# Layer boundary of a two-layer interaction network: grouped statistics, first operand spread by 0/1 matmuls, three keep-alive matmuls

## The chip, the cores and the metric

One core of a Trainium2 chip. The metric is the device time of one execution in microseconds (us), smaller is better; medians of several executions. All runs told here are of the same (fast) state. "Granted clock" is the share of TensorE's full clock that its throttle lets through, as the profile records it. DVE is VectorE, ACT ScalarE, PE TensorE, PEld its weight loads, SPq the queue from which SyncE issues DMAs.

## The reference, cut to what matters

```python
def _batchnorm(h, gamma, beta):                       # over rows and embedding
    mean = jnp.mean(h, axis=(0, 2), keepdims=True)
    var = jnp.var(h, axis=(0, 2), keepdims=True)
    return (h - mean) * rsqrt(var + EPS) * gamma + beta

def _cin_layer(out, x, W, b, gamma, beta):            # x: 4096 rows, 32 fields, 16
    h = einsum('rne,rfe->rnfe', out, x).reshape(r, -1, e)   # all products of pairs
    h = einsum('rce,oc->roe', h, W) + b
    return _batchnorm(h, gamma, beta)

h1 = _cin_layer(x, x, W1, b1, g1, beta1)              # 128 channels
out, direct1 = h1[:, :64], h1[:, 64:]
direct2 = _cin_layer(out, x, W2, b2, g2, beta2)
return concatenate([direct1, direct2], axis=1).sum(axis=-1)
```

The normalization of layer 1 needs the statistics of all of layer 1, so nothing of layer 2 can be multiplied before the last tile of layer 1 is done. The change is about this boundary.

## The kernel before

128 tiles of 512 columns per layer. In each tile VectorE multiplies two operands into z, TensorE multiplies z by the weights (fp32, two passes per matmul: 4096 passes recorded for layer 2's 2048 matmuls), ScalarE evicts the result, VectorE takes statistics. Layer 1's h (64 channels kept) stays in on-chip memory. At the boundary, all 128 tiles' statistics are aggregated by one instruction, and layer 2 takes its first operand a from h by DMA, one row spread over eight partitions:

```python
mv = const.tile([P, 2], ...)
nc.vector.bn_aggr(mv, stats.rearrange("p a b -> p (a b)"))   # 128 tiles x 6 numbers
...                                    # scale and shift: eight small steps
normalize(0)                           # ScalarE, h of the first tile
...
for t in range(NT):                    # layer 2
    b = bpool.tile([P, 4 * T], ...)
    nc.sync.dma_start(b, ...)          # 1 MB from HBM
    for i in range(4):
        a = apool.tile([P, T], ...)
        nc.sync.dma_start(a, src.unsqueeze(1).to_broadcast([16, 8, T]))   # from h
        z = zpool.tile([P, 4, T], ...)
        nc.vector.tensor_tensor(z, a (broadcast), b, ALU.mult)
        for k in range(4):
            nc.tensor.matmul(ps, w2_sb[:, m, :], z[:, k, :], ...)
```

The pools of layer 1 are closed before those of layer 2 are opened, so layer 2's buffers lie on memory that layer 1 has used, and wait for its last use (4.5 us on layer 1's last matmul, by the waits list). The first pool opened is that of layer 1's weights, and the first one of layer 2 lies where it lay:

```python
wpool = ...  # layer 1's weights
lpool = ...  # layer 1's loads
rpool = ...
...          # layer 2, later:
bpool = ...  # lies on wpool and lpool
```

## Time and profile before

| | before |
|---|---|
| time, median of 6 | 2289.79 us (2288.67 to 2290.40) |
| last matmul of layer 1 to first of layer 2 | 16.2 us |
| from there to the eviction of layer 2's first tile | 17.0 us, where a steady tile takes 13.73 |
| first tile's eviction to last tile's eviction of layer 2 | 1744.1 us |
| last tile's eviction to the end | 16.1 us |

The lines are shown in the prediction; in a timeline, the columns are start, duration, engine, line, operation, count, and in square brackets how long the engine stood idle before and what ended that.

### The profile page before, as it was taken

How to read it: one execution, taken by the hardware profiler on the slowest of the kernel's cores; microseconds unless marked ns; L12 is line 12 of the kernel's file. 1: busy time of each engine (PE TensorE's matmuls, PEld its weight loads, DVE VectorE, ACT ScalarE, POOL GpSimd, SP SyncE). 2: the span in 40 equal slices, each digit the busy share in tenths (PEclk: the TensorE clock that was granted, in tenths of full speed). 3: DMA queues.
4: the chain of work that ended last, by engine and by line, in shares of the span. 5: the costliest groups of instructions: out<-in, count | busy, mean ns of one | idle time of the engine just before them, and what ended most of it. 6: DMA issues, size and time to landing. Idle time of an engine off the chain costs nothing.

```text
span 2288.8 us, 15238 instructions
## 1 busy us (share of the span) xinstructions
PE 2245.0 (98%) x5376; PEld 982.4 (43%) x5376; DVE 1750.0 (76%) x1129; ACT 398.7 (17%) x580; POOL 2.3 (0%) x5
## 2 busy tenths in 40 slices
PE   8999999979999999999999999999999999999997
PEld 3444444434444444444444444444444444444443
DVE  6888888877777777777777777777777777777776
ACT  3555555556000000000000000000000000000000
POOL 0000000000000000000000000000000000000000
PEclk9999999989999999999999999999999999999998
DMA  8888888868888888888888888888888888888883
GB/s 316 298 305 295 298 292 301 296 201 158 153 150 151 153 154 155 155 150 151 153 157 155 154 150 151 152 158 154 154 150 151 152 159 154 154 149 151 152 155 92
DMA packets 132428, 417.05 MB, mean 182 GB/s; under 512 B 14848, under 2 KB 14848, under 8 KB 115456
## 3 DMA queue, kind: packets, MB, share of 16 engines
q1 hardware_dynamic: 131616, 413.20, 81.7%
q10 hardware_dynamic: 736, 2.89, 0.4%
q8 instruction: 42, 0.69, 0.1%
q14 instruction: 34, 0.28, 0.0%
HBM read 278.66 MB, written 3.15 MB: 123 GB/s over the span
## 4 chain that ended last, share of the span: by engine, by line
PE 77%; issue 22%; DVE 0%; ACT 0%; POOLq 0%; ACTq 0%; DVEq 0%
PE ps L211 77%; ACT h L177 0%; DVE mv L60 0%; POOLq L276 0%; ACTq L182 0%; DVE d L224 0%; DVEq L276 0%; ACT e L213 0%; DVE stats L214 0%; DVE d L215 0%; DVE ss L72 0%; DVE c L69 0%; ACT sd L64 0%; DVE r L66 0%; DVE ss L75 0%
## 5 line engine op out<-in xcount | busy, mean ns | idle before, releaser
L211 PE MATMUL ps<-z,w_sb 128*128 128x512 f32 x4096 | 1761.1, 593 | 16.2 <-ACT h L177 16.2
L208 DVE TENSOR_TENSOR z<-a,b 128x2048 f32<-128x2048 f32 x512 | 1173.0, 2291 | 446.4 <-PE ps L211 439.5
L211 PEld LDWEIGHTS ps<-z,w_sb 128*128 128x128 f32 x4096 | 779.2, 190 | 998.1 <-issue 980.8
L163 PE MATMUL ps<-z,w_sb 128*128 128x512 f32 x1024 | 450.9, 598 | 3.2 <-DVE z L151 3.2
L213 ACT ACTIVATE e<-ps,bn_sb 128x512 f32<-128x512 f32 x128 | 87.9, 687 | 1635.0 <-PE ps L211 1624.0
L151 DVE TENSOR_TENSOR z<-a,b 128x2048 f32<-128x2048 f32 x128 | 293.4, 2292 | 68.9 <-PE ps L163 65.0
L163 PEld LDWEIGHTS ps<-z,w_sb 128*128 128x128 f32 x1024 | 193.0, 191 | 259.6 <-issue 251.0
L129 ACT ACTIVATE e<-ps,bn_sb 128x512 f32<-128x512 f32 x128 | 87.9, 687 | 219.5 <-PE ps L163 219.5
L214 DVE BATCH_NORM_STATS2 stats<-e 128x6 f32<-128x512 f32 x128 | 87.7, 685 | 5.3 <-ACT e L213 5.3
L132 DVE BATCH_NORM_STATS2 stats<-e 128x6 f32<-128x512 f32 x128 | 87.8, 686 | 3.4 <-ACT e L129 3.4
L130 ACT ACTIVATE ed<-ps,bn_sb 64x512 f32<-64x512 f32 x128 | 87.4, 683 | 3.2
L131 ACT ACTIVATE h<-ps,bn_sb 64x512 f32<-64x512 f32 x128 | 87.2, 681 | 2.4
L215 DVE TENSOR_REDUCE d<-e 128x32 f32<-128x512 f32 x128 | 85.5, 668 | 0.0
L177 ACT ACTIVATE h<-h,keep 128x512 f32<-128x512 f32 x64 | 45.7, 800 | 3.8 <-issue 1.9
L161 PE MATMUL ps<-zr,w_sb 32*128 32x512 f32 x256 | 37.4, 655 | 8.1 <-DVE w_sb L115 8.1
L135 DVE TENSOR_REDUCE d<-ed 128x32 f32<-128x512 f32 x64 | 42.8, 668 | 0.0
L161 PEld LDWEIGHTS ps<-zr,w_sb 32*128 32x128 f32 x256 | 10.2, 186 | 31.7 <-issue 23.5
L148 DVE TENSOR_TENSOR zr<-r 128x512 f32<-128x512 f32 x16 | 10.9, 682 | 6.7 <-DMA r<-in_xr 6.7
L60 DVE BATCH_NORM_AGGREGATE mv<-stats 128x2 f32<-128x768 f32 x2 | 7.2, 3612 | 0.0
L129 ACT ACT_TABLE_LOAD x1 | 1.3, 1283 | 8.5 <-DMA bn_sb<-in_bn 8.5
L224 DVE TENSOR_SCALAR d<-d,ss 128x2048 f32<-128x2048 f32 x2 | 2.6, 1343 | 0.0
L180 POOL TENSOR_SCALAR d<-d,direct 128x2048 f32<-128x2048 f32 x1 | 2.0, 2048 | 503.3 <-DVE direct L174 503.3
(17 smaller groups left out, 6.7 us busy)
## 6 DMA issues: line engine op xcount, KB each, us to landing
b<-in_xb SPq DMA_DIRECT2D x128, 1024.0 KB, 7.2
a<-h SPq DMA_DIRECT2D x512, 256.0 KB, 5.2
a<-in_xa SPq DMA_DIRECT2D x128, 512.0 KB, 4.9
b<-in_xb SPq DMA_DIRECT2D x128, 512.0 KB, 5.6
r<-in_xr SPq DMA_DIRECT2D x16, 512.0 KB, 6.1
out<-d SPq DMA_DIRECT2D x2, 1024.0 KB, 4.5
w_sb<-in_w ACTq DMA_DIRECT2D x1, 1024.0 KB, 10.0
out<-d ACTq DMA_DIRECT2D x2, 512.0 KB, 8.9
```

What stands on the lines that cost most here:

```text
L129: nc.scalar.activation(e, ps, AF.Identity, bias=b1)
L130: nc.scalar.activation(ed[to, :], ps[KEEP:, :], AF.Identity, bias=b1[KEEP:])
L131: nc.scalar.activation(hs[c][to, :], ps[:KEEP, :], AF.Identity, bias=b1[:KEEP])
L132: nc.vector.bn_stats(stats1[:, t, :], e)
L151: nc.vector.tensor_tensor(z, a.rearrange("p (a t) -> p a t", a=2).unsqueeze(2).to_broadcast([P, 2, 2, T]), b.rearrange("p (b t) -> p b t", ...
L161: nc.tensor.matmul(ps, w1_sb[rows, 4 + s // 4, :], zr[rows, :], start=True, stop=False)
L163: nc.tensor.matmul(pss[t], w1_sb[:, m, :], z[:, m // 2, m % 2, :], start=False, stop=(m == 3))
L208: nc.vector.tensor_tensor(z, a.unsqueeze(1).to_broadcast([P, 4, T]), b, ALU.mult)
L211: nc.tensor.matmul(ps, w2_sb[:, m, :], z[:, k, :], start=(m == 0), stop=(m == 15))
L213: nc.scalar.activation(e, ps, AF.Identity, bias=b2)
L214: nc.vector.bn_stats(stats2[:, t, :], e)
L215: nc.vector.tensor_reduce(d2[half][:, c * RT : (c + 1) * RT], e.rearrange("p (r e) -> p r e", e=EMB), AX.X, ALU.add,)
```

## The change

Its intent: shorten the path between the layers and at the end. Statistics are aggregated per 16 tiles, so that only a short aggregation is left at the end; the last tile's statistics come straight from PSUM; the small steps are fewer; the first tile's four a are made by TensorE itself, by matmuls with a 0/1 matrix of 64 rows into PSUM (called spreads below), in place of a DMA; three matmuls whose result is not used (keep-alive) are to keep the array's clock up; the direct sums are scaled later.

```diff
+        def add(self, t, h, bias=None):
+            ...
+            nc.vector.bn_stats(self.stats[:, t % SG, :], h)
+            ...
+            if t % SG == SG - 1:
+                nc.vector.bn_aggr(self.groups[:, t // SG, 1:3], self.stats...)
...
+    running = psum.tile([P, T], FP, tag="ps", name="running")
+    for k in range(3):
+        nc.tensor.matmul(running, w2_sb[:, k, :], w2_sb[:, 0:4, :]..., start=True, stop=True)
...
-    normalize(0)
-    nc.gpsimd.tensor_scalar(d1, d1, direct[:, 0:1], direct[:, 2:3], ALU.mult, ALU.add)
+    nc.vector.tensor_scalar(hs[0][low, :], hs[0][low, :], ss1[low, 0:1], ss1[low, 1:2], ...)
...
+    def spread(i):
+        a = psum.tile([P, T], FP, tag="ps", name="a_first")
+        return nc.tensor.matmul(a, select[:, i]..., hs[0][low, :], start=True, stop=True)
+    spread(0)
...
+            if t == 0:
+                a = spreads[i]
+                if i == 0:
+                    spread(1)
+            else:
+                nc.sync.dma_start(a, src.unsqueeze(1).to_broadcast([16, 8, T]))
+            for js in ([slice(0, 1), slice(1, 4)] if t == 0 and i == 0 else [slice(0, 4)]):
...
+                if t == 0 and m in (0, 3):
+                        spread(2 + m // 3)
```

`low` is partitions 0 to 63. A square root of a constant at the very start loads ScalarE's table early (1.28 us).

More of the change, by code (lines that the diff above doesn't have):

```diff
@@ L38 @@
 GROUP = 8
+SG = 16
 @with_exitstack
@@ L47, in tile_cin @@
     sums = ctx.enter_context(tc.tile_pool(name="sums", bufs=1))
+    spool = ctx.enter_context(tc.tile_pool(name="spool", bufs=2))
     epool = ctx.enter_context(tc.tile_pool(name="epool", bufs=2))
@@ L55, in load_bn @@
         return bn_sb
-    def batchnorm(stats, gamma, beta, n):
-        mv = const.tile([P, 2], FP, tag=f"mv{n}", name=f"mv{n}")
-        nc.vector.bn_aggr(mv, stats.rearrange("p a b -> p (a b)"))
-        ve = const.tile([P, 1], FP, tag=f"ve{n}", name=f"ve{n}")
-        nc.vector.tensor_scalar(ve, mv[:, 1:2], EPS, None, ALU.add)
-        sd = const.tile([P, 1], FP, tag=f"sd{n}", name=f"sd{n}")
-        nc.scalar.activation(sd, ve, AF.Sqrt)
-        r = const.tile([P, 1], FP, tag=f"r{n}", name=f"r{n}")
-        nc.vector.reciprocal(r, sd)
-        c = const.tile([P, 1], FP, tag=f"c{n}", name=f"c{n}")
-        nc.vector.tensor_scalar(c, r, r, ve, ALU.mult, ALU.mult)
-        nc.vector.tensor_scalar(c, c, -0.5, 1.5, ALU.mult, ALU.add)
-        ss = const.tile([P, 3], FP, tag=f"ss{n}", name=f"ss{n}")
-        nc.vector.tensor_scalar(ss[:, 0:1], r, c, gamma, ALU.mult, ALU.mult)
-        ms = const.tile([P, 1], FP, tag=f"ms{n}", name=f"ms{n}")
-        nc.vector.tensor_tensor(ms, mv[:, 0:1], ss[:, 0:1], ALU.mult)
-        nc.vector.tensor_tensor(ss[:, 1:2], beta, ms, ALU.subtract)
-        nc.vector.tensor_scalar(ss[:, 2:3], ss[:, 1:2], float(EMB), None, ALU.mult)
-        return ss
+    eps = const.tile([P, 1], FP, tag="eps", name="eps")
@@ new lines, in tile_cin, with __init__, scale_shift @@
+    nc.vector.memset(eps, EPS)
+    nc.scalar.activation(const.tile([P, 1], FP, tag="sd", name="table"), eps, AF.Sqrt)
+    class Stats:
+        def __init__(self, n):
+            self.n = n
+            self.groups = const.tile([P, NT // SG, 3], FP, tag=f"groups{n}", name=f"groups{n}")
+            nc.vector.memset(self.groups, 1.0)
+        def add(self, t, h, bias=None):
+            if t % SG == 0:
+                self.stats = spool.tile([P, SG, 6], FP, tag="stats", name=f"stats{self.n}")
+            nc.vector.bn_stats(self.stats[:, t % SG, :], h)
+            if bias is not None:
+                means = self.stats[:, t % SG, 1:5:3]
+                nc.vector.tensor_scalar(means, means, bias, None, ALU.add)
+            if t % SG == SG - 1:
+                nc.vector.bn_aggr(self.groups[:, t // SG, 1:3], self.stats.rearrange("p a b -> p (a b)"))
+        def scale_shift(self, gamma, beta):
+            mv = const.tile([P, 2], FP, tag="mv", name="mv")
+            nc.vector.bn_aggr(mv, self.groups.rearrange("p a b -> p (a b)"))
+            sd = const.tile([P, 1], FP, tag="sd", name="sd")
+            root = nc.scalar.activation(sd, mv[:, 1:2], AF.Sqrt, bias=eps)
+            half_ve = const.tile([P, 1], FP, tag="ve", name="half_ve")
+            nc.vector.tensor_scalar(half_ve, mv[:, 1:2], EPS, 0.5, ALU.add, ALU.mult)
+            r = const.tile([P, 1], FP, tag="r", name="r")
+            nc.vector.reciprocal(r, sd)
+            c = const.tile([P, 1], FP, tag="c", name="c")
+            nc.vector.tensor_scalar(c, r, r, half_ve, ALU.mult, ALU.mult)
+            nc.vector.scalar_tensor_tensor(c, c, 1.5, r, ALU.subtract, ALU.mult, reverse0=True)
+            ss = const.tile([P, 3], FP, tag=f"ss{self.n}", name=f"ss{self.n}")
+            nc.vector.tensor_tensor(ss[:, 0:1], c, gamma, ALU.mult)
+            nc.vector.scalar_tensor_tensor(
+                ss[:, 1:2], mv[:, 0:1], ss[:, 0:1], beta, ALU.mult, ALU.subtract, reverse1=True
+            )
+            return ss, root.ins
@@ L80, in tile_cin @@
+    select = const.tile([KEEP, 4, 16, 8], FP, tag="select", name="select")
+    nc.gpsimd.memset(select, 1.0)
+    nc.gpsimd.affine_select(
+        out=select,
+        in_=select,
+        pattern=[[-16, 4], [-1, 16], [0, 8]],
+        compare_op=ALU.is_equal,
+        fill=0.0,
+        base=0,
+        channel_multiplier=1,
+    )
     hs = [hpool.tile([P, T], FP, tag=f"h{c}", name=f"h{c}") for c in range(NC)]
     d1 = sums.tile([P, ROWS // 2], FP, tag="sum", name="d1")
-    stats1 = const.tile([P, NT, 6], FP, tag="stats", name="stats1")
+    stats1 = Stats(1)
@@ L127, in finish, with evict_direct, sum_direct @@
             ed = eds[c]
-            e = epool.tile([P, T], FP, tag="e", name="e")
-            nc.scalar.activation(e, ps, AF.Identity, bias=b1)
-            nc.scalar.activation(ed[to, :], ps[KEEP:, :], AF.Identity, bias=b1[KEEP:])
+            if t == NT - 1:
+                stats1.add(t, ps, b1)
+            else:
+                e = epool.tile([P, T], FP, tag="e", name="e")
+                nc.scalar.activation(e, ps, AF.Identity, bias=b1)
+                stats1.add(t, e)
             nc.scalar.activation(hs[c][to, :], ps[:KEEP, :], AF.Identity, bias=b1[:KEEP])
-            nc.vector.bn_stats(stats1[:, t, :], e)
+            if t == NT - 1:
+                return ps
+            evict_direct(ed[to, :], ps)
             if half == 1:
-                del eds[c]
-                nc.vector.tensor_reduce(
-                    d1[:, c * RT : (c + 1) * RT],
-                    ed.rearrange("p (r e) -> p r e", e=EMB),
-                    AX.X,
-                    ALU.add,
-                )
+                sum_direct(c)
+        def evict_direct(ed, ps):
+            nc.scalar.activation(ed, ps[KEEP:, :], AF.Identity, bias=b1[KEEP:])
+        def sum_direct(c):
+            nc.vector.tensor_reduce(
+                d1[:, c * RT : (c + 1) * RT],
+                eds.pop(c).rearrange("p (r e) -> p r e", e=EMB),
+                AX.X,
+                ALU.add,
+            )
         zr = None
@@ L165, in tile_cin @@
                 finish(t - 1)
-        finish(NT - 1)
-    ss1 = batchnorm(stats1, g1, beta1, 1)
-    keep = const.tile([P, 2], FP, tag="keep", name="keep")
-    direct = const.tile([P, 3], FP, tag="direct", name="direct")
-    for half in range(2):
-        to = slice(half * KEEP, (half + 1) * KEEP)
-        nc.vector.tensor_copy(keep[to, :], ss1[:KEEP, 0:2])
-        nc.vector.tensor_copy(direct[to, :], ss1[KEEP:, :])
-    def normalize(c):
-        nc.scalar.activation(hs[c], hs[c], AF.Identity, scale=keep[:, 0:1], bias=keep[:, 1:2])
@@ L179, in tile_cin @@
-    normalize(0)
-    nc.gpsimd.tensor_scalar(d1, d1, direct[:, 0:1], direct[:, 2:3], ALU.mult, ALU.add)
-    for half in range(2):
-        nc.scalar.dma_start(
-            out[:KEEP, half * (ROWS // 2) : (half + 1) * (ROWS // 2)],
-            d1[half * KEEP : (half + 1) * KEEP, :],
-        )
+        last = finish(NT - 1)
+    running = psum.tile([P, T], FP, tag="ps", name="running")
+    for k in range(3):
+        nc.tensor.matmul(
+            running, w2_sb[:, k, :], w2_sb[:, 0:4, :].rearrange("p a b -> p (a b)"), start=True, stop=True
+        )
@@ new lines, in tile_cin, with normalize @@
+    ss1, root1 = stats1.scale_shift(g1, beta1)
+    keep = const.tile([P, 2], FP, tag="keep", name="keep")
+    direct = const.tile([P, 2], FP, tag="direct", name="direct")
+    low, high = slice(0, KEEP), slice(KEEP, P)
+    nc.vector.tensor_scalar(hs[0][low, :], hs[0][low, :], ss1[low, 0:1], ss1[low, 1:2], ALU.mult, ALU.add)
+    nc.vector.tensor_copy(keep[high, :], ss1[low, 0:2])
+    nc.vector.tensor_copy(keep[low, :], ss1[low, 0:2])
+    def normalize(c, rows=slice(0, P)):
+        nc.scalar.activation(
+            hs[c][rows, :], hs[c][rows, :], AF.Identity, scale=keep[rows, 0:1], bias=keep[rows, 1:2]
+        )
@@ new lines, in tile_cin, with write_direct @@
+    with tc.issue_after(root1):
+        evict_direct(eds[NC - 1][high, :], last)
+    normalize(0, high)
+    def write_direct():
+        sum_direct(NC - 1)
+        nc.vector.tensor_scalar(ss1[high, 2:3], ss1[high, 1:2], float(EMB), None, ALU.mult)
+        for half in range(2):
+            nc.vector.tensor_copy(direct[half * KEEP : (half + 1) * KEEP, :], ss1[high, 0:3:2])
+        nc.scalar.activation(d1, d1, AF.Identity, scale=direct[:, 0:1], bias=direct[:, 1:2])
+        for half in range(2):
+            nc.scalar.dma_start(
+                out[:KEEP, half * (ROWS // 2) : (half + 1) * (ROWS // 2)],
+                d1[half * KEEP : (half + 1) * KEEP, :],
+            )
@@ L191, in tile_cin @@
     d2 = [pool.tile([P, ROWS // 2], FP, tag="sum", name=f"d2_{half}") for half, pool in enumerate((late, sums))]
-    stats2 = const.tile([P, NT, 6], FP, tag="stats", name="stats2")
+    stats2 = Stats(2)
+    spreads = []
+    def spread(i):
+        a = psum.tile([P, T], FP, tag="ps", name="a_first")
+        spreads.append(a)
+        return nc.tensor.matmul(
+            a, select[:, i].rearrange("k n f -> k (n f)"), hs[0][low, :], start=True, stop=True
+        )
+    spread(0)
     for t in range(NT):
@@ L203, in tile_cin @@
         for i in range(4):
-            src = hs[c][half * KEEP + 16 * i : half * KEEP + 16 * (i + 1), :]
-            a = apool.tile([P, T], FP, tag="a", name="a")
-            nc.sync.dma_start(a, src.unsqueeze(1).to_broadcast([16, 8, T]))
             z = zpool.tile([P, 4, T], FP, tag="z", name="z")
-            nc.vector.tensor_tensor(z, a.unsqueeze(1).to_broadcast([P, 4, T]), b, ALU.mult)
+            if t == 0:
+                a = spreads[i]
+                if i == 0:
+                    spread(1)
+            else:
+                src = hs[c][half * KEEP + 16 * i : half * KEEP + 16 * (i + 1), :]
+                a = apool.tile([P, T], FP, tag="a", name="a")
+                nc.sync.dma_start(a, src.unsqueeze(1).to_broadcast([16, 8, T]))
+            for js in ([slice(0, 1), slice(1, 4)] if t == 0 and i == 0 else [slice(0, 4)]):
+                n = js.stop - js.start
+                made = nc.vector.tensor_tensor(
+                    z[:, js, :], a.unsqueeze(1).to_broadcast([P, n, T]), b[:, js, :], ALU.mult
+                )
             for k in range(4):
                 m = 4 * i + k
-                nc.tensor.matmul(ps, w2_sb[:, m, :], z[:, k, :], start=(m == 0), stop=(m == 15))
+                multiplied = nc.tensor.matmul(ps, w2_sb[:, m, :], z[:, k, :], start=(m == 0), stop=(m == 15))
+                if t == 0 and m in (0, 3):
+                    with tc.issue_after(multiplied.ins):
+                        spread(2 + m // 3)
+            if t == 0 and i == 1:
+                with tc.issue_after(made.ins):
+                    write_direct()
         e = epool.tile([P, T], FP, tag="e", name="e")
         nc.scalar.activation(e, ps, AF.Identity, bias=b2)
-        nc.vector.bn_stats(stats2[:, t, :], e)
+        stats2.add(t, e)
         nc.vector.tensor_reduce(
@@ L220, in tile_cin @@
         )
-    ss2 = batchnorm(stats2, g2, beta2, 2)
+    ss2, _ = stats2.scale_shift(g2, beta2)
+    nc.vector.tensor_scalar(ss2[:, 2:3], ss2[:, 1:2], float(EMB), None, ALU.mult)
     for half in range(2):
```

## The prediction

> **What bounds the kernel now.** I read the page first, for where the array waits; then the timeline at the border between the layers and at the end; then the windows for the granted clock.
>
> ```profile
> PE 2245.0 (98%) x5376; PEld 982.4 (43%) x5376; DVE 1750.0 (76%) x1129; ACT 398.7 (17%) x580; POOL 2.3 (0%) x5
> ...
> L211 PE MATMUL ps<-z,w_sb 128*128 128x512 f32 x4096 | 1761.1, 593 | 16.2 <-ACT h L177 16.2
> ```
>
> TensorE is busy for 98% of the span, and layer 2 alone is 1761.1 us in 4096 passes (two passes for each of 2048 fp32 matmuls), one per 0.43 us. Its only recorded idle time is 16.2 us, once. The change doesn't touch those passes, so it can only win in that hole, in the slow passes behind it, at the start (13.4 us until the first product of z) and at the end (16.2 us from the last matmul, at 2272.6, to 2288.8). Together these are 49 us with the 3.3 us derived below, 2.1% of the time.
>
> The hole, in the timeline (start, duration, engine, line, operation):
>
> ```profile
> 495.33 1.21 SPq L200 DMA_DIRECT2D b<-in_xb  x2
> 495.34 0.69 ACT L129 ACTIVATE e<-ps,bn_sb 128x512 f32<-128x512 f32 x1 [1.34 <-PE ps L163]
> ...
> 497.37 3.61 DVE L60 BATCH_NORM_AGGREGATE mv<-stats 128x2 f32<-128x768 f32 x1
> ...
> 509.15 2.29 DVE L208 TENSOR_TENSOR z<-a,b 128x2048 f32<-128x2048 f32 x1 [5.55 <-DMA a<-h]
> ...
> 511.54 1.19 PE L211 MATMUL ps<-z,w_sb 128*128 128x512 f32 x1 [16.24 <-ACT h L177]
> ```
>
> The array stops at 495.30 (call it T0). Eviction, statistics and sum of the last tile take until 497.4, aggregation until 501.0, the small steps until 503.2, normalization until 504.1, the load of the first a until 509.15, and a whole z until 511.44. The page names ACT for the wait of 16.2 us; the chain shows that VectorE and a DMA hold most of it. I note the first line too: layer 2's first two loads of b leave only at 495.33. Their buffers lie where layer 1's weights lay, and they wait for the last layer-1 matmul (the waits list 4.5 us on it).
>
> The clock, in windows (stretch, busy time of each engine, granted clock, DMA share, GB/s):
>
> ```profile
> 500.00:501.00 1.00, 0.00 (x0) 0.00 (x0) 0.98 (x1) 0.00 (x0) 0.00 (x0) 0.72 1.10 229
> 501.00:502.00 1.00, 0.00 (x0) 0.00 (x0) 0.65 (x4) 0.20 (x1) 0.00 (x0) 0.50 0.87 180
> ...
> 517.40:517.50 0.10, 0.10 (x1) 0.00 (x0) 0.00 (x0) 0.10 (x1) 0.00 (x0) 0.50 0.80 184
> 517.50:517.60 0.10, 0.10 (x2) 0.02 (x1) 0.00 (x0) 0.10 (x1) 0.00 (x0) 0.97 0.78 205
> ```
>
> The clock falls to half at 500.4 and is full again at 517.5, so layer 2 starts cold. Its first tile is evicted at 528.57; from T0 that is 33.2 us = 16.24 of hole + 32 passes x 0.429 = 13.73 + 3.3 lost to the slow clock.
>
> The end:
>
> ```profile
> 2274.60 3.61 DVE L60 BATCH_NORM_AGGREGATE mv<-stats 128x2 f32<-128x768 f32 x1
> 2278.25 0.15 DVE L62 TENSOR_SCALAR ve<-mv 128x1 f32<-128x1 f32 x1
> ...
> 2280.26 2.60 DVE L224 TENSOR_SCALAR d<-d,ss 128x2048 f32<-128x2048 f32 x2
> ```
>
> The aggregation is on the path in full, then 2.05 us of small steps; the scaling and the writes behind 2280.26 stay.
>
> [...]
>
> **The change at the border.** Estimates from T0; the handover of dependent VectorE steps costs some 0.04 each in the timeline.
> - The eviction of the last tile leaves the path: statistics straight from PSUM 0.69, bias added to the means 0.2.
> - Aggregation: 3.61 us for 768 elements is about 4.6 ns each with an assumed 0.1 fixed; so 96 elements 0.55, and 24 of the groups 0.2. These two sizes are extrapolated from one point.
> - Square root 0.2 with handover 0.27; reciprocal 0.2; the two steps of the correction 0.3 and 0.3; scale 0.2; shift 0.25: 1.5.
> - Rows 0 to 63 of the first h on VectorE, 64x512: 1.34 for 2048 elements scaled down to about 0.5.
> Sum with handovers: about 4.0 us; h is ready at T0 + 4.0 = 499.3. The first 0/1 matmul, two passes of 0.43 and its latency, gives a_0 at about 500.3. Without any other wait the first quarter of z (0.69 for 128x512) would be done at 501.0, and the hole be 5.8 us.
>
> But z also needs b, and b's order of waits is the same in both kernels: the changed kernel's list of instructions still makes the first b wait for the last matmul of layer 1. Leaving at 495.33 and taking 7.4, it lands at 502.73, 2.4 us after a_0. **So I expect b, not a, to end the wait.** The first quarter of z runs 502.75 to 503.45, and the first product of layer 2 starts at 503.5: 8.2 us after T0 instead of 16.24.
>
> TensorE in between: three keep-alive matmuls (2.6 us) until 497.9, two spreads about 499.4 to 501.1, then idle 2.4 us until 503.5. [...]the clock should stay full. Then first product 0.86, third spread 0.86 (to 505.2, where the other three quarters of z end), three products, fourth spread 0.86, and from there z keeps ahead: z_1 is ready at 507.5, and the sum and copies put behind it cost 1.2 us, which fits before z_2 is needed at 512. The loads of a for tile 1 queue behind the second b (about 507.4), and are wanted near 515. The scaling of d1 on ScalarE has a whole tile of room.
> From T0 to the end of the first tile: 8.2 + two spreads 1.72 + 13.73 = 23.65, against 33.2. **Border: -9.6 us** (hole -8.0, slow clock -3.3, spreads +1.7).
>
> **At the end.** From the last bn_stats to the aggregate: before 4.80 (2273.41 to 2278.21). After: 0.72 + 0.48 for 96 elements + 0.58 sum + 0.23 for 24 = 2.0, so -2.8. The small steps lose the addition of epsilon before the root and one product: 2.05 becomes 1.5 to 1.9. **End: -3.1 us.**
>
> **In the layers.** One aggregation of 0.55 per 16 tiles is added. In layer 1 a z of 2.29 may start 3.43 before it is needed, leaving 1.14 us; statistics, sum and aggregation are 1.9 together, once per 16 tiles, and the delay of about 0.8 is within that. Layer 2 has VectorE idle 446 us. So 0.
>
> **At the start.** The table load and the dummy root (1.5 us) now stand between ScalarE's first and second DMA issue, so w1m's issue slips from 1.19 to about 2.7. The first w1 landed only at 5.6, so the queue is still fed, and the first z waited for b until 11.06 while w1m's sum was done at 8.1. Moving 415 GB/s, the engines are full; the order may shift either way. 0, give or take 0.5.
>
> **Sum.** 2290.15 - 9.6 - 3.1 = 2277.45; with some 0.3 for a chance of the clock falling, 2277.7 us, 0.5% faster.
>
> **Rivals.**
> 1. b isn't what ends the wait, because it lands by 500.3 or its wait is released earlier. Then the hole is 5.8, and the time 2275.3. For it: that is plainly the design's aim. Against it: the 1 MB takes 7.2 us at the median of 128 loads, and its waits are unchanged.
> 2. The clock falls in spite of the keep-alive, since two spreads fill a little under a third of a window (500.4 to 503.9 at the phase of this trace). Whether so little activity counts isn't in this trace; a half-busy window, 493.6 to 497.0, did keep it. A fall would cost one cold window, 1.7 us, perhaps 3: 2279.4 to 2281.
> 3. The small steps are longer than my sums (instructions with a column as operand took 0.27, not 0.15; PSUM reads). Up to 2.4 us of that hides behind b, so only the end pays: +0.3 to +0.5.
> 4. A collision on SBUF or in the queues makes b slower, or the start loses the 1.5 us of the table load: 2279.
>
> **Range and chances.** Gains and losses of rivals give 2275.3 to 2281; runs of the kernel before differ by 0.9[...]. I take 2275.2 to 2280.5. A gain of 2% would need 45.8 us, nearly all of those 49: 1%. A loss of 2% has no candidate: below 1%.
>
> **What would show it.** First z of layer 2 recorded as waiting for the load of b, starting near 502.7, with the second spread long done; first layer-2 product 8.2 us behind the last of layer 1; granted clock 1.00 throughout; two aggregations near 0.55 and 0.2; 3 us less from the last layer-2 matmul to the end. I am wrong if z waits for the spread (rival 1), if the clock shows 0.50 after the border (rival 2), or if the first z of layer 1 starts a microsecond later than 11.06.

What the trace of the kernel before had: the clock is at half for 17.07 us and falls 5.1 us after the last matmul; the two loads of b land 7.4 and 11.5 us after their issue; a z of 2048 elements from SBUF takes 2.29 us; ScalarE's table load takes 1.28 us (from 497.45), beside the aggregation. A window in rival 2 is the step of 3.41 us at which the traces show the clock change (below), and its 1.7 us is half of it, the clock being 0.50.

## The result, and the profile after

| | median | range |
|---|---|---|
| before, 6 runs | 2289.79 us | 2288.67 to 2290.40 |
| after, 6 runs | 2282.26 us | 2281.32 to 2282.49 |

The ratio of after to before is 0.9967, 95% interval 0.9954 to 0.9979. Here and below a ratio is the mean time of one kernel's fast runs over that of the other's fast runs of the same rounds, so not quite the ratio of the medians. The change gains 7.5 us, not 12.4, and the time lies above the predicted range.

From the page of the kernel after, the line of layer 2's matmuls and that of the 0/1 matmuls:

```profile
L296 PE MATMUL ps<-z,w_sb 128*128 128x512 f32 x4096 | 1762.1, 594 | 2.2 <-DVE z L291 2.2
...
L265 PE MATMUL a_first<-h,select 64*128 64x512 f32 x8 | 5.1, 749 | 1.5 <-DVE h L227 1.5
```

The idle time of 16.2 us is gone: 2.2 and 1.5 are left. By this line alone one would expect the full gain. The timeline of the boundary in the kernel after:

```profile
494.08 1.21 SPq L276 DMA_DIRECT2D b<-in_xb  x2
...
495.08 0.59 DVE L81 BATCH_NORM_AGGREGATE groups<-stats 128x2 f32<-128x96 f32 x1
495.71 0.27 DVE L86 BATCH_NORM_AGGREGATE mv<-groups 128x2 f32<-128x24 f32 x1
...
498.17 1.95 PE L265 MATMUL a_first<-h,select 64*128 64x512 f32 x4 [1.54 <-DVE h L227]
...
501.45 4.55 DVE L291 TENSOR_TENSOR z<-a_first,b 128x512 f32<-128x512 f32 x3 [3.04 <-DMA b<-in_xb]
502.29 2.05 PE L296 MATMUL ps<-z,w_sb 128*128 128x512 f32 x2 [2.17 <-DVE z L291]
504.26 2.07 PE L265 MATMUL a_first<-h,select 64*128 64x512 f32 x2
...
506.26 5.37 PE L296 MATMUL ps<-z,w_sb 128*128 128x512 f32 x6
```

T0, the end of layer 1's matmuls, is 494.08 here (the issue of b, which waits for it). The a is there about 499; z starts only when b has landed, 7.4 us after T0, and the first product comes at 8.21 us. That is the predicted hole. But two passes of a product take 2.05 us and six 5.37, when six take 2.74 at full clock (the keep-alive passes from 493.89). The windows of the same stretch (length, busy time of PE, PEld, DVE, ACT and POOL, each with its number of instructions, then granted clock, DMA share, GB/s), cut in steps of 3.41 us from its changes (more on this step below):

```profile
497.73:501.14 3.41, 1.95 (x4) 0.67 (x4) 0.61 (x3) 2.87 (x4) 0.00 (x0) 1.00 1.00 223
501.14:504.56 3.42, 2.27 (x3) 0.80 (x4) 3.11 (x3) 3.42 (x6) 0.00 (x0) 0.50 1.00 217
504.56:507.97 3.41, 3.41 (x4) 1.04 (x4) 2.18 (x3) 3.41 (x6) 0.00 (x0) 0.50 1.02 247
507.97:511.38 3.41, 3.41 (x5) 1.01 (x3) 0.00 (x0) 0.39 (x1) 0.00 (x0) 0.50 0.86 213
```

The clock falls at 501.14, before the first product, and is back only at 511.38. The array is idle no longer than 2.2 us at a time, and it computes for 57% of the window after which the clock falls. In the last two of the four windows it is recorded as busy throughout, and yet the third, which holds a spread of 64 rows, doesn't bring the clock back.

The end of the kernel after:

```profile
2269.32 0.57 DVE L81 BATCH_NORM_AGGREGATE groups<-stats 128x2 f32<-128x96 f32 x1
2269.93 0.26 DVE L86 BATCH_NORM_AGGREGATE mv<-groups 128x2 f32<-128x24 f32 x1
...
2271.89 2.60 DVE L316 TENSOR_SCALAR d<-d,ss 128x2048 f32<-128x2048 f32 x2
```

The 3.61 us of the single aggregation became 0.57 and 0.26 on the path. Where the 8.1 us between the two profiled executions (2288.8 and 2280.7) lie:

| stretch | before | after | difference | predicted |
|---|---|---|---|---|
| start to T0 | 495.33 | 494.08 | -1.25 | 0 |
| T0 to eviction of layer 2's first tile | 33.24 | 29.14 | -4.10 | -9.6 |
| to eviction of its last tile | 1744.12 | 1744.18 | +0.06 | 0 |
| to the end | 16.11 | 13.30 | -2.81 | -3.1 |

The -1.25 is not the change's. In every trace the clock's changes lie at whole multiples of 3.413 us from the first rise (141 of them to the fall in the kernel before, 142 in the one after; from there to the rise 5 in the first, 17.07 us, and 3 in the second, 10.24), and that first rise, in the first tile of layer 1, comes at another time in each execution: 19.15 us before, 16.45 after. The kernel with grouped aggregation alone (below), whose start is the old one, has it at 17.70 and T0 at 494.59. In all twelve profiles T0 less half of the time of the first rise is 485.6 to 486.1, so T0 follows the clock's phase, that is, where its 3.413 us steps (windows, below) lie in the execution. The missing gain is in the second row.

### The profile page after: what moved, and what is told of

Its sections match the earlier page's. It is cut to its first block, busy times and chain, and to the rows that moved or that the text cites. A ratio compares the mean times of both kernels' runs of the same rounds, so it can differ in the third digit from the quotient of the medians.

```text
span 2280.7 us, 15262 instructions
## 1 busy us (share of the span) xinstructions
PE 2252.1 (99%) x5390; PEld 986.2 (43%) x5390; DVE 1752.1 (77%) x1149; ACT 391.9 (17%) x580; POOL 1.8 (0%) x6
## 4 chain that ended last, share of the span: by engine, by line
PE 98%; DMA 1%; DVE 0%; DVEq 0%; SPq 0%; ACT 0%; issue 0%; ACTq 0%
PE ps L296 77%; PE ps L211 20%; PE ps L209 1%; DMA a<-in_xa 0%; DMA b<-in_xb 0%; PE a_first L265 0%; DVE z L199 0%; DVE d L316 0%; DVEq L368 0%; DVE z L291 0%; ACT e L304 0%; DVE stats L76 0%; SPq L139 0%; DVE d L306 0%; DVE groups L81 0%
## 5 line engine op out<-in xcount | busy, mean ns | idle before, releaser
L232 ACT ACTIVATE h<-h,keep 128x512 f32<-128x512 f32 (+1 forms) x64 | 45.7, 802 | 1.3 <-DVE keep L228 1.2
L291 DVE TENSOR_TENSOR z<-a_first,b 128x2048 f32<-128x2048 f32 (+2 forms) x5 | 9.1, 1860 | 10.0 <-PE ps L296 6.9
L81 DVE BATCH_NORM_AGGREGATE groups<-stats 128x2 f32<-128x96 f32 x16 | 9.3, 578 | 0.0
L265 PE MATMUL a_first<-h,select 64*128 64x512 f32 x8 | 5.1, 749 | 1.5 <-DVE h L227 1.5
```

Of the source, the lines that this page charges most:

```text
L232: nc.scalar.activation(hs[c][rows, :], hs[c][rows, :], AF.Identity, scale=keep[rows, 0:1], bias=keep[rows, 1:2])
L291: made = nc.vector.tensor_tensor(z[:, js, :], a.unsqueeze(1).to_broadcast([P, n, T]), b[:, js, :], ALU.mult)
```

## The experiments

Nine kernels were run, one of them in two batches, so ten runs, each timed five times and profiled once. Theories, put up for testing: **A**, whether the clock holds depends on how many rows of the array the matmuls use; **B**, it depends only on the share of time in which the array is busy. **C**, the load of a takes a fixed 5 us from its issue; **D**, it queues behind the second load of b. The mean granted clock of an execution tells them roughly apart: 0.998 where it held over the border, 0.996 or less where it was down for long; 0.997 lies between, and there the time tells. Clauses of the expectations of the first two runs that gave rows a weight, or a share of time a limit, are cut where marked: no run measured either.

| kernel | median us | ratio to before, interval | mean clock in its 5 runs |
|---|---|---|---|
| after (for comparison, 6 runs) | 2282.26 | 0.9967, 0.9954 to 0.9979 | five 0.996, one 0.997 |
| spreads of 128 rows | 2277.83 | 0.9951, 0.9938 to 0.9963 | 0.998 three times, 0.997, 0.996 |
| filled, 128 rows | 2278.50 | 0.9952, 0.9939 to 0.9964 | all 0.998 |
| filled, 64 rows | 2278.73 | 0.9953, 0.9941 to 0.9966 | all 0.998 |
| b early | 2276.61 | 0.9955, 0.9941 to 0.9969 | three 0.998, two 0.996 |
| both | 2276.09 | 0.9939, 0.9926 to 0.9953 | all 0.998 |
| no keep-alive | 2282.37 | 0.9967, 0.9955 to 0.9980 | 0.995 or 0.996 |
| groups only | 2285.73 | 0.9982, 0.9970 to 0.9995 | 0.994 or 0.995 |
| no spread | 2283.26 | 0.9972, 0.9960 to 0.9985 | four 0.996, one 0.995 |
| 64 rows, same times | 2282.70 | 0.9971, 0.9958 to 0.9983 | four 0.996, one 0.995 |
| spreads of 128 rows, again | 2277.75 | 0.9949, 0.9936 to 0.9963 | four 0.998, one 0.997 |

All of them are faster than before by less than 2%, and all gave a right result.

### Spreads of 128 rows

```diff
-    select = const.tile([KEEP, 4, 16, 8], FP, tag="select", name="select")
+    select = const.tile([P, 4, 16, 8], FP, tag="select", name="select")     # rows 64 to 127 are 0
-    nc.vector.tensor_scalar(hs[0][low, :], hs[0][low, :], ss1[low, 0:1], ss1[low, 1:2], ...)
     ...                                                                      # copies to keep
+    nc.vector.tensor_scalar(hs[0], hs[0], keep[:, 0:1], keep[:, 1:2], ALU.mult, ALU.add)
-    normalize(0, high)
-            a, select[:, i]..., hs[0][low, :], start=True, stop=True
+            a, select[:, i]..., hs[0], start=True, stop=True
```

> The 0/1 matmuls take all 128 rows (64 of weights zero) and VectorE normalizes all of the first h; nothing else changes. Theory A[...]: [...]the window with them is at least as active as the half-busy one that kept the clock in the kernel before, the granted clock stays 1.00 across the border, first product still 8.2 us after the last matmul of layer 1 (b ends the wait), time near 2277 (5 less than the changed kernel). Theory B[...]: the clock falls as in the changed kernel, time 2281 to 2282.

Measured: 2277.83 us, four of five runs near 2278 and one at 2280.24 with a mean clock of 0.996. A window of the profiled run:

```profile
498.80:502.21 3.41, 1.96 (x4) 0.68 (x4) 0.41 (x2) 3.41 (x6) 0.00 (x0) 1.00 1.03 228
```

It has 1.96 us of the same four passes as the window of the kernel after that had 1.95 and was followed by the fall; the clock stays at 1.00. From T0 to the eviction of the first tile are 23.88 us; predicted for a held clock were 23.65. So with the clock held, the prediction's working of the boundary is right to 0.3 us.

### Filled with keep-alive matmuls of 128 rows, and of 64

```diff
-    for k in range(3):
-        nc.tensor.matmul(running, w2_sb[:, k, :], w2_sb[:, 0:4, :]..., ...)
+    def keep_running(n): ...              # second kernel: w2_sb[:KEEP, ...] on both sides
+    keep_running(5)
...
                     spread(1)
+                    keep_running(2)
```

> Keep-alive matmuls of 128 rows fill the border: five instead of three before the first spread, two more between the second spread and the first product. Spreads stay at 64 rows. Theories A and B both: clock 1.00 throughout[...]; time 2277 to 2278. If it falls all the same, both are wrong.

> The same fill as in the run with 128 rows, in the same places and numbers, but the keep-alive matmuls use 64 rows of the array as the spreads do. Array busy in time as before. Theory A: the clock falls in the border in spite of a busy array, time 2281 to 2283. Theory B: it stays at 1.00, time 2277 to 2278.

Measured: 2278.50 and 2278.73, the clock held in all ten runs (mean clock 0.998). A window of the second's profiled run, filled with matmuls of 64 rows throughout:

```profile
497.93:501.35 3.42, 3.42 (x9) 1.48 (x8) 1.99 (x9) 2.11 (x4) 0.00 (x0) 1.00 1.05 252
```

The first agrees with both theories. The second contradicts what I had written for A: here a stream of 64-row matmuls that was busy for 3.42 of 3.42 us did hold the clock. What these runs leave of A is that rows went with the outcome where the array was busy for part of a window. It doesn't rescue B: at the same share of 57%, the 128-row spreads above held the clock (1.96 us, between gaps of 1.9 and 1.7 us) and the 64-row ones of the kernel after didn't (1.95). Both kernels are 0.7 to 0.9 us slower than that one though the clock is full (0.998). In the first, going from matmuls of 128 rows to ones of 64 and back took longer: from one product over the third spread to the next product, start to start, were 2.08 us (503.98 to 506.06) against 1.80 (502.83 to 504.63) with all at 128 rows.

### b early

```diff
-        wpool = one.enter_context(tc.tile_pool(name="wpool", bufs=1))
         lpool = one.enter_context(tc.tile_pool(name="lpool", bufs=3))
         rpool = one.enter_context(tc.tile_pool(name="rpool", bufs=1))
+        wpool = one.enter_context(tc.tile_pool(name="wpool", bufs=1))
```

> Only the order of three pools of layer 1 changes: the buffers of b in layer 2 now lie where layer 1's inputs lay and no longer on its weights, so the first b waits for VectorE's last z and not for the last matmul. Leaves 4.5 us earlier, lands about 3 us after the last layer-1 matmul. Then the spread ends the wait: first product 5.8 to 6.1 us after the last layer-1 matmul instead of 8.2. Time 2280 if the clock falls as in the changed kernel, 2275 to 2276 if the shorter border keeps it (theory B: shares of time rise; theory A: likelier to fall, since most activity in that window is spreads).

Measured: 2276.61 us; three runs near 2276.2, two near 2282.4. In the profiled run (one of the quicker three; T0 is 494.33):

```profile
499.56 4.55 DVE L291 TENSOR_TENSOR z<-a_first,b 128x512 f32<-128x512 f32 x3 [0.89 <-PE a_first L265]
500.39 1.10 PE L296 MATMUL ps<-z,w_sb 128*128 128x512 f32 x2
```

The first z now waits for the spread, and the first product comes 6.06 us after T0 instead of 8.21. So b was the bound of the hole, as the prediction said, and three lines in another order remove it. The two other runs, 6 us off, have a mean clock of 0.996 where the other three have 0.998, in one and the same kernel with 64-row spreads: the expectations of 2275 to 2276 and of 2280 each describe some of the runs, the first up to 0.6 us too low and the second by 2.

### Both repairs

The two changes above and five keep-alive matmuls instead of three.

> The changed kernel with both repairs: spreads of 128 rows and b's buffers on layer 1's inputs, with five keep-alive matmuls instead of three, so that they reach to the first spread. Expected if rows count and b was the bound: clock 1.00 across the border in every run, first product about 6.3 us after the last layer-1 matmul (h is ready 0.35 later than in the changed kernel, since the copies of scale and shift come first), no run above 2278, median 2275.5. If runs above 2280 appear as in the run with b early alone, the clock still falls and rows are not the cause.

Measured: 2276.09 us, all runs between 2275.45 and 2276.43, clock 0.998 in all. First product 6.45 us after T0 (501.16 less 494.71), first tile evicted 22.17 after T0. This beats both kernels: 13.6 us below the median of the kernel before in the same rounds (2289.65), and 6.2 below the changed one's median, which comes from other rounds. In the profile the matmuls of layer 2 have no idle time left.

### No keep-alive

```diff
-    running = psum.tile([P, T], FP, tag="ps", name="running")
-    for k in range(3):
-        nc.tensor.matmul(running, ...)
```

> The changed kernel without its three keep-alive matmuls. If the fall of the clock there is due to the window with the two 64-row spreads, the keep-alive only delays the fall by one window, while nothing but spreads runs: time 2282 to 2283, no worse than the changed kernel by more than 1 us. If the keep-alive is worth what it was meant for, 2285 or more.

Measured: 2282.37 us, the time of the changed kernel. So the three keep-alive matmuls of the change, as placed, bought nothing. The windows show why it costs nothing either to leave them out, and they show something on the way back up:

```profile
495.49:498.90 3.41, 0.15 (x1) 0.18 (x2) 2.89 (x12) 1.64 (x4) 0.00 (x0) 1.00 0.89 209
498.90:502.32 3.42, 3.42 (x4) 0.84 (x4) 0.55 (x2) 3.40 (x5) 0.00 (x0) 0.50 1.04 230
502.32:505.73 3.41, 3.11 (x5) 1.00 (x4) 3.41 (x3) 3.41 (x6) 0.00 (x0) 0.50 0.95 208
505.73:509.14 3.41, 3.41 (x5) 1.17 (x4) 1.43 (x3) 3.21 (x5) 0.00 (x0) 0.50 1.07 263
```

The clock falls one window earlier, and in the next window only the two spreads run, twice as long, while b is awaited anyway. That window is full of 64-row matmuls, and the clock doesn't rise; it rises after the last one, which is mostly 128-row products. In these two profiles, then, a full window of 64 rows held a full clock (497.93 to 501.35 in the run filled with 64, 3.42 us busy) and didn't raise a fallen one (498.90 to 502.32 here, 3.42).

### Groups only, and no spread

The first is the kernel before with the aggregation by 16 tiles and nothing else. The second is the changed kernel with the first four a loaded by DMA:

```diff
-            if t == 0:
-                a = spreads[i]
-                ...
-            else:
-                a = apool.tile(...)
-                nc.sync.dma_start(a, ...)
+            a = apool.tile(...)
+            nc.sync.dma_start(a, ...)
```

> The kernel before with the grouped aggregation alone. End: 2.8 us less. Border, theory C (the load of a takes a fixed 5 us from its issue, as the timeline of before suggests): the hole shrinks by the same 2.8, time 2283.9. Theory D (a queues behind the second load of b, which lands 12 us after the last layer-1 matmul, so an earlier issue gains little): the hole shrinks by 1.0 to 1.5, time 2285.5.

> The changed kernel with the first four a loaded by DMA again, everything else kept. h is ready 4 us after the last layer-1 matmul instead of 8.8. Theory C: a lands 9.2 us after it, first product at 11.5, clock fallen: time about 2282. Theory D: a lands only about 13 us after it, behind the second b; first product at 15 to 15.6 instead of 16.2: time 2285 to 2286, so all savings in the arithmetic of the border together gain less than 1 us without the spreads.

Measured: 2285.73 and 2283.26 us. Groups only is D's 2285.5 in time, though its hole shrank by 0.6 us (15.68 against 16.24) and not by D's 1.0 to 1.5. Its boundary, and below it that of no spread:

```profile
500.91 18.82 SPq L221 DMA_DIRECT2D a<-h  x9
...
507.84 4.49 DVE L223 TENSOR_TENSOR z<-a,b 128x2048 f32<-128x2048 f32 x2 [7.44 <-DMA a<-h]
510.24 9.98 PE L226 MATMUL ps<-z,w_sb 128*128 128x512 f32 x16 [15.68 <-ACT h L192]
```

```profile
498.02 18.46 SPq L260 DMA_DIRECT2D a<-h  x9
...
507.32 4.56 DVE L263 TENSOR_TENSOR z<-a,b 128x512 f32<-128x512 f32 x3 [8.94 <-DMA a<-h]
508.15 12.26 PE L268 MATMUL ps<-z,w_sb 128*128 128x512 f32 x24 [11.56 <-DVE z L263]
```

Their T0 are 494.59 and 494.06. The loads of a leave 6.3 and 4.0 us after it, and a is used 13.25 and 13.26 us after it. An issue that is 2.3 us earlier gains nothing: behind the two loads of b, the second of which lands 12.1 us after T0 (issue at 0.6, 11.5 to landing), a arrives when the queue has worked them off. In the kernel before, with the a issued 8.8 us after T0, it was 13.8. So D holds for what a costs, and C falls. The time of no spread contradicts what I wrote for D, by 2 us in its favour: the quarter of z as first piece puts the product 0.8 us behind a where a whole z took 2.4 (14.1 after T0, expected 15 to 15.6), and the clock, which had fallen, was back 3.5 us after the first product, where the kernel before took 6.0. What the spreads really remove is a queue: 8.21 us to the first product instead of 14.1. The two spreads behind it, the longer slow clock and the switching between row counts take nearly all of that back (2282.26 against 2283.26).

### 64 rows at the same times, and 128 rows again

The shift of the spreads by 0.35 us in the run with 128 rows was a loose end. The first kernel is that one with `select` of 64 rows and `hs[0][low, :]` again; the second is that one itself, on the same chip.

> The run with 128-row spreads in everything, its later spreads too, except that the spreads take 64 rows again. If the number of rows decides whether the clock holds, it falls in at least 4 of 5 runs (mean clock 0.996) and the time is 2282 to 2283. If it was the shift of the spreads by 0.35 us that kept the clock in that run, it holds in 4 of 5 and the time is 2278.

> The 128-row spreads once more, on the same chip and in the same rounds as the run with 64 rows at the same times. Rows decide: clock 0.998 in at least 4 of 5 runs, median 2277 to 2278.5, some 4 us below the 64-row run. Otherwise: within 1 us of it.

Measured: 2282.70 and 2277.75; the clock was low in all five runs of the first, and 0.998 in four of the second. By luck both profiles have the same phase. First 64 rows, then 128:

```profile
497.15:500.56 3.41, 1.49 (x5) 0.44 (x4) 2.28 (x11) 2.19 (x4) 0.00 (x0) 1.00 1.01 245
500.56:503.98 3.42, 3.29 (x5) 1.14 (x4) 1.39 (x2) 3.42 (x6) 0.00 (x0) 0.50 1.04 220
503.98:507.39 3.41, 3.41 (x4) 0.50 (x2) 3.41 (x3) 3.41 (x6) 0.00 (x0) 0.50 0.97 212
```

```profile
497.16:500.58 3.42, 1.50 (x4) 0.49 (x3) 2.37 (x11) 2.10 (x4) 0.00 (x0) 1.00 0.92 230
500.58:503.99 3.41, 2.90 (x4) 0.67 (x2) 0.68 (x2) 3.41 (x6) 0.00 (x0) 0.50 1.03 219
503.99:507.40 3.41, 3.25 (x8) 1.60 (x9) 3.41 (x3) 3.41 (x6) 0.00 (x0) 1.00 0.97 204
```

In this phase both kernels fell, after a window that was busy for 44%, most of it keep-alive. With 128 rows the next window, less busy than the other kernel's (2.90 us against 3.29), brings the clock back at 503.99, before the first product starts at 504.15. With 64 rows it stays down until 510.80. Same times, same phase, other rows: in these two kernels the clock goes with the number of rows, or with something that changes with it (see what stays open, below).

## Why the prediction was right or wrong

The prediction was wrong: it forecast 2277.7 us with a clock that holds across the border; the clock fell there, and 2282.26 was measured.

- **b ends the wait, first product 8.2 us after T0.** Right: 8.21, with z waiting for b by the trace, and 6.06 when b is made to come early. Rival 1 fell.
- **"The clock should stay full."** This is the step that failed. The slow stretch of the first tile was 5.96 us long before (511.54 to 517.50), and 9.09 after (502.29 to 511.38); at the clock of 0.50 recorded there half of it is lost, 3.0 us and 4.5 us. So the loss that I took off stayed, and 1.5 came on top. (My 3.3 was what a subtraction left over. Only 3.0 of it was the clock; the other 0.3 is there at full clock too, see the spreads below.) I had reasoned from the length of idle gaps alone, and no run showed that to be the measure: the clock fell in the kernel after with no gap above 2.2 us, and held with spreads of 128 rows and gaps of 1.9 and 1.7 us. Beside a shift of the spreads by 0.35 us, what differed between these two was the rows, in windows of 3.41 us with 1.95 and 1.96 us of work. The trace of before told of one half-busy window of 128 rows that kept the clock (1.70 of 3.42 us), and I carried it over to one filled by 64.
- **Rival 2**, that the clock falls in spite of the keep-alive, was named with "so little activity", and mis-sized: 1.7, perhaps 3. It cost 5.26 us, the measured 29.14 less the 23.88 of the run with spreads of 128 rows and a held clock: 4.55 of slow clock and 0.71 left over. I attribute that 0.71 to the four changes between 64 and 128 rows: at full clock they cost 0.78 (the filled kernels, from first product to first tile's eviction, 16.51 against 15.73 with all at 128 rows); at half clock it was not measured by itself. So the kernel with 64-row spreads lost time twice, and the prediction had neither.
- **Spreads, 1.7 us.** Right as busy time: with 128 rows and full clock the boundary is 23.88 where 23.65 was predicted. From first product to first eviction it has 15.73, 0.28 more than 13.73 + 1.72: the 0.3 that I had counted as slow clock.
- **Border -9.6 us.** With the clock as it was, -4.1; without the fault, 23.88 less 33.24 is -9.4.
- **End -3.1 us.** -2.8. The aggregations of 96 and 24 elements were put at 0.55 and 0.2 and measured 0.57 to 0.59 and 0.26 (with the 3.61 for 768, I estimate some 0.15 us fixed and 4.5 ns per element); from the last bn_stats (2268.12) to the aggregate's end (2270.19) are 2.07, predicted 2.0. The small steps took 1.70 from there to the scaling at 2271.89, within the 1.5 to 1.9. Up to the scaling the sum is -3.1 as predicted (3.77 us from the last bn_stats against 6.85); what is missing lies behind it, where scaling and writes, which I took as fixed, took 8.81 us instead of 8.54. The two kernels of groups only and no spread had 8.56 and 8.54, so this is not the change's either.
- **In the layers, 0.** Right: layer 2 from its first eviction to its last differs by 0.06 us.
- **At the start, 0.** Right in kind: the second weights' issue didn't even slip as the instruction list suggested (1.32 in the profile, while the table loaded), and the first z started at 11.25. That the profiled T0 came 1.25 us earlier is the clock's phase.
- **Rival 3**, longer small steps, has nothing for it at the end, and at the border the wait for b would have hidden it. **Rival 4** has nothing for it: b took 7.4 as before.

What stays open is what the clock goes by; no run shows a rule. Three windows of 128-row work, the first and the last from the kernel before, the second from the end of the changed kernel:

```profile
493.60:497.02 3.42, 1.70 (x4) 0.39 (x3) 0.95 (x2) 2.03 (x4) 0.00 (x0) 1.00 0.21 36
...
2265.84:2269.25 3.41, 1.48 (x4) 0.38 (x2) 1.13 (x2) 0.69 (x1) 0.00 (x0) 1.00 0.00 0
...
510.67:514.08 3.41, 2.54 (x3) 1.17 (x4) 2.06 (x2) 3.41 (x6) 0.00 (x0) 0.50 0.95 254
```

By recorded busy time, the clock held through windows of 128-row work that were busy for 50% (the first), for 57% (498.80 to 502.21 with spreads of 128 rows) and for 43% (the second: the clock falls only one window later, at 2272.66, after one without any matmul); after one of 44% it fell (497.16 to 500.58, the second run with spreads of 128 rows). The ends of matmuls are modelled in these shares, so 43% and 44% can't be told apart, and no limit is read from them. With 64-row work the clock held in full windows (the run filled with 64) and fell after one of 57% (497.73 to 501.14 in the kernel after). A fallen clock stayed down after 128-row windows of 70% (509.21 to 512.63 in groups only) and 74% (the third) and after a full one of 64 rows (498.90 to 502.32 without keep-alive), and rose after one of 128 rows and 85% (500.58 to 503.99, the second run with spreads of 128 rows). No run measured what a 64-row matmul is worth beside a 128-row one, and other counts of rows weren't tried. Nor was it separated whether the rows or the data moved into them make the difference; the 64 added rows had weights of zero, so the spreads' results are the same.

## What to carry to other kernels

When a wait is cut short at a boundary, look up what the memory of the next stage's buffers waits for: here another order of three pool lines took 2.2 us off the hole, while issuing a's loads 2.3 us earlier on a full queue took off nothing. For a matmul that bridges a gap, try all 128 rows of the array: here the same spreads with 128 rows, half of them zeros, ran in 2277.83 and 2277.75 us, with 64 rows in 2282.26 and 2282.70. Don't take a short gap for a safe one: the clock fell here with none above 2.2 us. And check the granted clock on both sides of the place: here the idle time of TensorE at the boundary went from 16.2 to 3.7 us on the page, while the slow stretch of the first tile grew from 5.96 to 9.09 us.
